# Layer 3 of a four-layer graph network on one core: constants made in layer 2, rank comparisons summed on TensorE, 1/std applied after the projection, blocks in a written-out order

## The chip, the core and the metric

The kernel runs on one core of a Trainium2 chip. The metric is the device time of the core in microseconds. Before the change the median of three runs is 767.4 us (766.89 to 767.92). The execution that the profiler recorded took 764.35 us, of which 762.5 us lie between its first and its last instruction (the span). The mean clock that TensorE was granted in it is 0.952 of full speed.

## The reference

Four layers work on `x` (2708 nodes, 128 features) and a 0/1 matrix `adj` (2708 x 2708). Each is `x = x + layer(relu(layernorm(x)))`. The first three (an attention layer, a graph convolution, a mean aggregation with batch normalisation) are not touched. The last one, with `X = relu(layernorm(x))`, is

```python
XW = jnp.matmul(X, W)
s_col = jnp.matmul(XW, a[0, :f])
s_row = jnp.matmul(XW, a[0, f:])
Z1 = jax.nn.leaky_relu(s_row[:, None] + s_col[None, :], negative_slope=0.01)
den = jnp.exp(Z1)
num = jnp.matmul(A, den)
att = jnp.where(num != 0, den / jnp.where(num != 0, num, 1.0), 0.0)
H = jnp.matmul(A, jnp.matmul(att, XW))
```

and layer normalisation is `(x - m) / sqrt(v + eps)` over the 128 features.

## The kernel before, in words

The nodes are cut into 22 tiles of 128 (the last has 20), and the tiles into six blocks of four (the last block has two). Layers 0 to 2 stream `adj` and its transpose and multiply on TensorE (PE) by block. Layers 1 and 2 are driven by a list of slots, four passes of 22 tiles: for each slot the kernel prepares a cast adjacency tile (L483 on VectorE, DVE; L481 on ScalarE, ACT), issues its matmuls (L614), and then runs whatever small steps were put at that tick (`put`, L498). In a slot of layer 2's first pass there are eight matmuls of 512 columns. All of it lies in an `in_order()` section (L236): within it each engine executes its instructions as the program writes them. Outside such a section a scheduler picks the order.

Layer 3 does not form the 2708 x 2708 exponentials row by row. It sorts nodes by their score `s_row` (in the code `r_of`), cuts the sorted order into chunks of 124, and takes sums of exponentials by chunk. So it needs the rank of each node: how many nodes have a larger score, ties broken by index. This is how the stage between layer 2 and the sorting works:

- Layer 2 ends with batch statistics: `tot` gets mean and variance (L833), 1/std (L834, a power on GpSimd, POOL, at L157), scale and offset (L835 to L837).
- Then come the constants of layer 3 (L862 to L912): five index patterns on POOL and some forty small instructions on DVE.
- `refresh(b)` (L990): ACT makes `z`, the normalised layer-2 result of a block (L997); PE turns it (L184); DVE adds it to `xs` (L1001); then `layernorm` (L164): statistics on DVE (L167, L168), 1/std by the power on POOL (L157), `shift` on DVE (L172), and the scaled and shifted relu `h` on ACT (L174).
- `project(b)` (L1012): PE turns `h` (L180), ACT copies it to `hT` (L1018), PE multiplies by the weight with two score columns (L1025, two tiles to a PSUM bank), ACT copies the scores `r_of` and `c_col` (L1026, L1027), takes `c_scale` = exp(0.01 c) (L1028) and scales the values `xw` (L1031), which SP stores (L1032). DVE spreads the scores onto a diagonal (`diag`, L1037), PE multiplies it by ones (L1044), and ACT copies the product to `row_b` (L1045): every partition then holds the scores of the whole block in a row.
- `ranks(b)` (L965): for each tile t of the block, DVE compares `row_b` of all earlier tiles with the tile's own scores (`bits`, L972; L978 for the first five, where DVE sums as well). For tiles after the fifth, ACT sums the bits by row in a pass of its own (`junk`, L974, into `rowsum`). PE sums the bits by column into `rk` with a weight that picks one row per block (L985).
- `diagonal(b)` (L953): the same within a tile, with the strict upper triangle `before`, the row sum read out into `tied` (L957), and the column sum on PE (L961).
- The scores are split into bf16 pieces (L1059), `rk` is copied and turned (L1083, L1086), `below` = others - rowsum - tied (L1087, L1088), and the rank is `below` plus the column count (L1092 to L1098). `less` (L1100), the weights `wts` (L1106, L1107), and the whole planning of chunks and gathers follow from the rank.

In this stage the scheduler, not the program text, sets the order. For instance it runs the `refresh` of all blocks well ahead of the projections. `bits` has three buffers, `bank` two PSUM banks; banks `acc0` to `acc5` are single.

Of the kernel before, what the change touches and what calls it, by code (L numbers as in the profile page):

```python
# [20 lines left out]
def binary(  # L21
# [21 lines left out]
    nc = tc.nc  # L43
# [675 lines left out]
    with in_order():  # L719
# [48 lines left out]

        lay_pool = tc.tile_pool(name="lay", bufs=2, side="right", reuse_waits="tile")
# [43 lines left out]

        NTAIL2 = 3
# [20 lines left out]
    nc.vector.tensor_mul(tot[:, 5:6], vecs[:, 2:3], tot[:, 4:5])  # L835
    nc.vector.scalar_tensor_tensor(tot[:, 2:3], tot[:, 0:1], -1.0, tot[:, 5:6], ALU.mult, ALU.mult)
    nc.vector.tensor_add(tot[:, 6:7], tot[:, 2:3], vecs[:, 3:4])  # L837

    CH = P - 4
    NC = T  # L840
    NE = T
    NS = 2 * NE
    NW = NC - 1
    NV = 5
    FAR_DOWN = float(1 << 16)
# [3 lines left out]

    const3 = ctx.enter_context(tc.tile_pool(name="const3", bufs=1, side="right"))  # L850

    def iota(name, shape, pattern, mult, base=0):
        o = const3.tile(shape, F32, name=name)
        nc.gpsimd.iota(o, pattern, base=base, channel_multiplier=mult, allow_small_or_imprecise_dtypes=True)
        return o

    def const_op(name, shape, op, *args, dtype=F32):
        o = const3.tile(shape, dtype, name=name)
        op(o, *args)
        return o  # L860

    node = iota("node", [P, T], [[P, T]], 1)  # L862
    by_ch = iota("by_ch", [P, NC + 1], [[CH, NC + 1]], 0)
    lane = iota("lane", [P, P], [[1, P]], 0)
    part = iota("part", [P, 1], [[0, 1]], 1)
    others = iota("others", [P, T], [[P, T]], -1, base=P - 1)
    nc.vector.tensor_scalar_add(others[:, TF:], others[:, TF:], float(TAIL - P))
    ts_ = nc.vector.tensor_scalar
    valid = const_op("valid", [P, T], ts_, node, float(N), None, ALU.is_lt)
    far = const_op("far", [P, T], ts_, valid, -1.0, 3.0e4, ALU.add, ALU.mult)  # L870
    lane_b = const_op("lane_b", [P, P], nc.vector.tensor_copy, lane, dtype=BF16)
    ones_b = const3.tile([P, P], BF16, name="ones_b")
    nc.vector.memset(ones_b, 1.0)
    before = const_op("before", [P, P], ts_, lane, part, None, ALU.is_gt, dtype=BF16)
    b_of = const3.tile([P, 1], F32, name="b_of")
    v_of = const3.tile([P, 1], F32, name="v_of")
    ge_v = const_op("ge_v", [P, NV], ts_, by_ch[:, :NV], float(NC) / CH, None, ALU.mult)
    nc.vector.tensor_tensor(ge_v, part.to_broadcast([P, NV]), ge_v, ALU.is_ge)
    nc.vector.tensor_reduce(v_of, ge_v[:, 1:], AX.X, ALU.add)
    nc.vector.scalar_tensor_tensor(b_of, v_of, float(-NC), part, ALU.mult, ALU.add)  # L880
    is_b = const_op("is_b", [P, NC], ts_, lane[:, :NC], b_of, None, ALU.is_equal)
    b_next = const_op("b_next", [P, P], ts_, ones, part, 1.0, ALU.mult, ALU.add)
    is_r = const_op("is_r", [P, 1], ts_, v_of, 3.0, None, ALU.is_lt)
    is_n = const_op("is_n", [P, 1], ts_, v_of, 3.0, None, ALU.is_ge)
    first = const3.tile([P, P], F32, name="first")
    nc.vector.memset(first, 0.0)
    nc.vector.memset(first[0:1, :], 1.0)
    joint = const3.tile([P, 2 * NC], F32, name="joint")
    nc.vector.memset(joint, 0.0)
    for i in range(3):  # L890
        row_of = small.tile([P, 1], F32, tag="row_of", name="row_of")
        ts_(row_of, part, float(1 - 2 * NW * i), None, ALU.add)
        hit = small.tile([P, 2 * NW], F32, tag="hit", name="hit")
        ts_(hit, lane[:, 1 : 2 * NW + 1], row_of, None, ALU.is_equal)
        nc.vector.tensor_add(joint[:, 1 : 2 * NW + 1], joint[:, 1 : 2 * NW + 1], hit)
    is_lo = const3.tile([P, 1], F32, name="is_lo")
    is_hi = const3.tile([P, 1], F32, name="is_hi")
    for o, m in ((0, is_lo), (1, is_hi)):
        ts_(m, part, float(CH + o), None, ALU.is_equal)
        two = const_op(f"two{o}", [P, 1], ts_, part, float(CH + 2 + o), None, ALU.is_equal)  # L900
        nc.vector.tensor_add(m, m, two)
    slope_hi = const_op("slope_hi", [P, 1], ts_, is_lo, -0.99, 1.0, ALU.mult, ALU.add)
    slope_lo = const_op("slope_lo", [P, 1], ts_, is_hi, 0.99, 0.01, ALU.mult, ALU.add)
    tiny = const3.tile([P, 1], F32, name="tiny")
    nc.vector.memset(tiny, 1e-18)
    up = const_op("up", [P, 1], ts_, part, float(NC), None, ALU.mult)
    pick_b = const3.tile([P, NB, NB], BF16, name="pick_b")
    nc.vector.memset(pick_b, 0.0)
    for b in range(NB):
        nc.vector.memset(pick_b[:, b, b : b + 1], 1.0)  # L910
    none_b = const3.tile([P, NB], BF16, name="none_b")
    nc.vector.memset(none_b, 0.0)  # L912
# [30 lines left out]
    r_of = row("r_of", T)  # L943
    c_col = row("c_col", T)
    c_scale = row("c_scale", T)
    rowsum = row("rowsum", T)
    nc.vector.memset(rowsum, 0.0)
    tied = row("tied", T)
    nc.vector.memset(tied, 0.0)
    rk = acc_bank(5)  # L950
    nc.tensor.matmul(rk[:NB, :], none_b, ones_b[:, None, :].to_broadcast([P, 4, P]), start=True, stop=False)

    def diagonal(b):  # L953
        for q, t in enumerate(TILES[b]):
            r = rows(t)
            own = tabs.tile([P, P], BF16, tag="own", name="own", bufs=4)
            nc.vector.scalar_tensor_tensor(  # L957
                own[:r, :r], row_b[:r, vcols(t)], r_of[:r, t : t + 1], before[:r, :r], ALU.is_ge, ALU.mult,
                accum_out=tied[:r, t : t + 1],
            )  # L960
            nc.tensor.matmul(  # L961
                rk[:NB, q * P : q * P + r], pick_b[:r, b, :], own[:r, :r], start=False, stop=(t == T - 1)
            )

    def ranks(b):  # L965
        for t in TILES[b]:
            if not t:
                continue
            r = rows(t)
            bits = tabs.tile([P, N], BF16, tag="bits", name="bits", bufs=3)  # L970
            if t > 5:
                ts_(bits[:r, : t * P], row_b[:r, : t * P], r_of[:r, t : t + 1], None, ALU.is_gt)  # L972
                junk = tabs.tile([P, N], BF16, tag="junk", name="junk", bufs=1)
                nc.scalar.activation(  # L974
                    junk[:r, : t * P], bits[:r, : t * P], AF.Identity, accum_out=rowsum[:r, t : t + 1]
                )
            else:
                ts_(  # L978
                    bits[:r, : t * P], row_b[:r, : t * P], r_of[:r, t : t + 1], None, ALU.is_gt, ALU.add,
                    accum_out=rowsum[:r, t : t + 1],  # L980
                )
            for k in range(NB):
                x0, x1 = E0[k][0], min(E0[k][1], t * P)
                if x1 > x0:
                    nc.tensor.matmul(rk[:NB, : x1 - x0], pick_b[:r, k, :], bits[:r, x0:x1], start=False, stop=False)  # L985
        diagonal(b)

    h3s, xws3 = {}, {}

    def refresh(b):  # L990
        lo, hi = E0[b]
        n = len(TILES[b])
        ts = tiles_of(b)
        z = tabs.tile([P, 512], F32, tag="z", name="z")
        if hi - lo < n * P:
            nc.gpsimd.memset(z[:, hi - lo :], 0.0)
        nc.scalar.activation(z[:, : hi - lo], row_b[:, lo:hi], AF.Relu, bias=tot[:, 6:7], scale=tot[:, 5:6])  # L997
        p = acc_bank(b % 2)
        turned_flat(p, z, b)
        f = len([t for t in TILES[b] if t < TF])  # L1000
        nc.vector.tensor_add(  # L1001
            xs[:, ts.start : ts.start + f, :].rearrange("p t d -> p (t d)"),
            xs[:, ts.start : ts.start + f, :].rearrange("p t d -> p (t d)"),
            p[:, : f * P],
        )
        if f < n:
            nc.vector.tensor_add(xs[:TAIL, TF, :], xs[:TAIL, TF, :], p[:TAIL, cols(f)])
        h3 = tabs.tile([P, 4, P], F32, tag="h3", name="h3")
        layernorm(b, h3)
        h3s[b] = h3  # L1010

    def project(b):  # L1012
        n = len(TILES[b])
        ts = tiles_of(b)
        p = acc_bank(2 + b % 2)
        turned(p, h3s.pop(b), b)
        hT = tabs.tile([P, 512], F32, tag="hT", name="hT")
        nc.scalar.copy(hT[:, : n * P], p[:, : n * P])  # L1018
        xw = tabs.tile([P, 4, P], F32, tag="xw", name="xw")
        for half in range(0, n, 2):  # L1020
            p = bank()
            us = slice(ts.start + half, ts.start + half + 2)
# [26 lines left out]
    for b in range(NB):  # L1049
        if b + 1 < NB:  # L1050
            refresh(b + 1)
        project(b)
        if b:
            ranks(b - 1)
# [978 lines left out]
```

## Time and profile before

| | us |
|---|---|
| median of three runs | 767.4 |
| the profiled execution | 764.35 |
| its span | 762.5 |
| last product of layer 2 (L679) ends | 325.6 |
| `tot` is done on DVE (L837) | 329.8 |
| first comparison on DVE (L978) | 349.25 |
| last row sum on ACT (L974) ends | 391.7 |
| `below` (L931 for L1087) starts | 391.75 |
| first gather of layer 3's main loop (L1380) | 418.97 |

Over the whole span PE is busy 655.9 us (86%), DVE 588.8 (77%), ACT 467.7 (61%), POOL 243.8 (32%). These shares are means over stages with different limits; the stage of the change lasts from 325.6 to 391.75 us, 9% of the span, and is to be read from stretches of its own. Times in the trace count from the span's start. A matmul's recorded time includes its tail, so matmuls in a row overlap: what one costs is the distance from start to start. A line can be a helper's: L859, for instance, stands for most constants, and L931 for every `tt(...)`. In a timeline, equal instructions in a row are merged and shown with their number (x5), and the time is that of the group.

### The profile page before, as it was taken

The page shows a single profiled execution, that of the slowest core. Times are in us where ns is not written, and L with a number is a line of the kernel's source. Part 1 is how long each engine was busy: PE and PEld are TensorE (multiplying, and loading weights), DVE is VectorE, ACT ScalarE, POOL GpSimd, SP SyncE. Part 2 cuts the span into 40 slices and gives each one's busy share as a digit, 9 for nine tenths or more (in the row PEclk, how much of TensorE's full clock was granted, in tenths as well). Part 3 has the DMA queues.
Part 4 walks back from the last instruction along what each step waited for, and adds up shares of the span by engine and source line. Part 5 has one row for each costly group of instructions (what it writes and reads, how often), then busy time and mean ns, then how long its engine had stood idle before and what let it go on. Part 6 is the DMA issues. An engine that isn't in the chain of part 4 may idle for free. (4 is left out here: it accounts for less than half of the span.)

```text
span 762.5 us, 8134 instructions
## 1 busy us (share of the span) xinstructions
PE 655.9 (86%) x2626; PEld 411.8 (54%) x2626; DVE 588.8 (77%) x1102; ACT 467.7 (61%) x702; POOL 243.8 (32%) x201
## 2 busy tenths in 40 slices
PE   5889888888899989858739848899999999999995
PEld 3433333335778767634317525566655666557784
DVE  5999778968857874677789758678897887867972
ACT  5666677648956744447960139678766777664442
POOL 3320000141101100021000547788787787500000
PEclk9999999999999999968979969999999999999997
DMA  9699999577442899001000425556766555758702
GB/s 335 259 395 420 426 424 395 216 266 280 158 185 60 308 344 330 0 1 41 29 7 1 116 76 153 161 155 166 168 148 177 146 146 137 167 204 317 268 27 63
DMA packets 49733, 146.27 MB, mean 192 GB/s; under 512 B 13602, under 2 KB 28446, under 8 KB 41254
## 3 DMA queue, kind: packets, MB, share of 16 engines
q1 hardware_dynamic: 28966, 85.11, 31.5%
q0 software_dynamic: 16032, 25.83, 12.7%
q10 hardware_dynamic: 4684, 34.73, 12.6%
q8 instruction: 23, 0.38, 0.2%
q14 instruction: 28, 0.23, 0.1%
HBM read 126.81 MB, written 18.77 MB: 191 GB/s over the span
## 5 line engine op out<-in xcount | busy, mean ns | idle before, releaser
L1512 PE MATMUL bank<-r,d_hi 128*128 128x512 f32 (+1 forms) x264 | 143.7, 549 | 20.2 <-DMA r<-pre_d,pre_i 11.1
L1513 ACT ACTIVATE ln<-bank,tiny 128x512 f32<-128x512 f32 x132 | 83.8, 635 | 66.7 <-DVE e L1491 37.6
L1466 PE MATMUL acc<-e,xw 128*128 128x512 f32 (+1 forms) x264 | 121.5, 548 | 0.0
L340 PE MATMUL acc<-tau,hw 128*128 128x512 f32 (+1 forms) x240 | 101.1, 566 | 12.9 <-DVE tau L348 12.8
L1512 PE MATMUL bank<-r,d_lo 128*128 128x512 f32 (+1 forms) x264 | 99.2, 380 | 0.0
L1458 DVE CAST r<-g 124x2708 fp32r<-124x2708 fp8e4 x44 | 69.4, 1612 | 35.7 <-issue 17.1
L1380 POOL DMA_INDIRECT g<-adjt_d,row_i x44 | 84.5, 1921 | 39.1 <-DVE row_i L1304 26.0
L481 ACT CAST m<-a 128x660 fp32r<-128x660 fp8e4 (+1 forms) x45 | 55.2, 1234 | 51.9 <-PE acc L1628 31.6
L1512 PEld LDWEIGHTS bank<-r,d_hi 128*128 128x128 f32 x264 | 51.0, 193 | 62.2 <-issue 32.1
L340 PEld LDWEIGHTS acc<-tau,hw 128*128 128x128 f32 x240 | 43.8, 194 | 71.6 <-issue 46.5
L348 DVE SCALAR_TENSOR_TENSOR tau<-row_b,sg,a 128x1536 f32<-128x1536 f32 (+1 forms) x44 | 70.7, 1623 | 10.7 <-DMA a<-in_adj_dram 9.9
L1380 POOL DMA_INDIRECT r<-pre_d,pre_i x44 | 63.6, 1445 | 40.8 <-PE bank L1512 19.5
L1491 DVE SCALAR_TENSOR_TENSOR e<-row_b,sig,ln 128x1536 f32<-128x1536 f32 (+3 forms) x46 | 71.4, 1559 | 6.1 <-PE bank L1512 4.5
L371 ACT ACTIVATE a<-a 128x2708 fp8e4<-128x2708 f32 x22 | 54.1, 2459 | 23.1 <-issue 10.9
L695 DVE SCALAR_TENSOR_TENSOR chk<-chk 128x2708 f32<-128x2708 f32 (+1 forms) x22 | 65.7, 2987 | 3.0 <-DMA chk<-in_adj_t_dram 3.0
L1512 PEld LDWEIGHTS bank<-r,d_lo 128*128 128x128 f32 x264 | 51.1, 194 | 28.5 <-issue 24.2
L157 POOL TENSOR_TENSOR rstd<-isq,neg_half 128x4 f32<-128x4 f32 (+1 forms) x24 | 27.9, 1164 | 117.1 <-DVE isq L156 96.3
L1485 ACT ACTIVATE ln<-ln 128x512 f32<-128x512 f32 (+2 forms) x68 | 62.8, 926 | 0.7 <-ACT ln L1513 0.7
L483 DVE CAST m<-a 128x2048 fp32r<-128x2048 fp8e4 (+1 forms) x43 | 39.5, 920 | 23.1 <-PE acc L614 12.9
L1466 PEld LDWEIGHTS acc<-e,xw 128*128 128x128 f32 x264 | 48.1, 190 | 12.7 <-issue 3.8
L614 PE MATMUL acc<-m,y_hi 128*128 128x512 f32 (+1 forms) x132 | 49.8, 384 | 5.6 <-DVE m L600 2.0
L614 PE MATMUL acc<-m,h_hi 128*128 128x512 f32 (+1 forms) x132 | 53.9, 415 | 0.1
(440 smaller groups left out, 1251.0 us busy)
## 6 DMA issues: line engine op xcount, KB each, us to landing
a<-in_adj_dram SPq DMA_DIRECT2D x21, 1354.0 KB
adjt<-in_adj_t_dram ACTq DMA_DIRECT2D x12, 1354.0 KB
chk<-in_adj_t_dram ACTq DMA_DIRECT2D x11, 1354.0 KB
chk<-in_adj_t_dram SPq DMA_DIRECT2D x10, 1354.0 KB
a<-in_adj_t_dram SPq DMA_DIRECT2D x9, 1354.0 KB
adj_d<-a POOLq DMA_DIRECT2D x22, 338.5 KB
adjt_d<-adjt SPq DMA_DIRECT2D x5, 1354.0 KB
a<-adj_d SPq DMA_DIRECT2D x5, 1024.0 KB
```

What stands on the lines that cost most here:

```text
L340: nc.tensor.matmul(accs[b][:, : hi - lo], stationary, tau[b // 3][:, o : o + hi - lo], start=first, stop=last)
L348: nc.vector.scalar_tensor_tensor(tau, row_b[:, h0:h1], sg[:, t : t + 1], tiles_a[t][:, h0:h1], ALU.max, ALU.mult)
L481: nc.scalar.copy(m[:, : hi - lo], src[:, lo:hi])
L614: nc.tensor.matmul(sums_of[phase, b][:, : hi - lo], part[:, t, :], tiles_m[k][:, lo - base : hi - base], start=t == 0 and i == 0, stop=t = ...
L695: lambda: nc.vector.scalar_tensor_tensor(a[:r], a[:r], 1.0, a[:r], ALU.is_equal, ALU.not_equal, accum_out=odd[:r, t : t + 1])
L1380: return nc.gpsimd.indirect_dma_start(out=out, out_offset=None, in_=src, in_offset=bass.IndirectOffsetOnAxis(ap=idx, axis=0),)
L1458: ins = nc.vector.tensor_copy(rows_r[q][:CH], g[:CH])
L1466: m = nc.tensor.matmul(ys_acc[b][:, : hi - lo], xws[s], waiting[s][:, lo:hi], start=(s == 0), stop=(s == NE - 1))
L1485: pin(nc.scalar.activation(lns[s][:, lo:hi], lns[s][:, lo:hi], AF.Exp, scale=-1.0))
L1491: nc.vector.scalar_tensor_tensor(waiting[s][:, lo:hi], row_b[:, lo:hi], sig[:, s : s + 1], lns[s][:, lo:hi], ALU.max, ALU.mult)
L1512: pin(nc.tensor.matmul(num[:, : hi - lo], d, a[:, lo:hi], start=(i == 0), stop=(i == 3)))
L1513: pin(nc.scalar.activation(lns[s][:, lo:hi], num[:, : hi - lo], AF.Ln, bias=tiny))
```

## The change

Four things are done.

1. The constants of layer 3 are put into layer 2's slots: `later` collects one instruction each, and `put(l2_tick + 2 + i, make)` places one at each tick from layer 2's first pass on. `first` goes, a bf16 identity `ident_b` is new.
2. 1/std of the last layer normalisation no longer scales `h`. `centred` takes relu(x - mean) only, and 1/std is multiplied into the scores (`scores`, on DVE, straight from PSUM) and into the values' factor (`factors`: the exponential on ACT, a multiplication on POOL, then `values3` on ACT). The copies of `r_of` and `c_col` on ACT go.
3. The row sums of the comparisons go to PE. `compared(t)` writes the strict and the diagonal comparison into one `bits` tile; PE adds it up by column as before, and then adds its t+1 pieces of 128 columns onto each other with `ident_b` as the weight, in one PSUM bank (`folds`, acc3) for the four tiles of a block. `row_sums(b)` on DVE reduces that bank. The ACT pass, the sums on DVE and `tied` go.
4. The whole stage stands in an `in_order()` section, whose order is written out. The explicit load of the activation table ahead of the stage goes.

The diff, cut to its core:

```diff
+        later = []
...
+        def const_op(name, shape, op, *args, dtype=F32):
+            o = cell(name, shape, dtype)
+            later.append(lambda: op(o, *args))
+            return o
...
+        ident_b = const_op("ident_b", [P, P], nc.vector.tensor_copy, ident, dtype=BF16)
...
+        for i, make in enumerate(later):
+            put(l2_tick + 2 + i, make)
...
-    rk = acc_bank(5)
-    nc.tensor.matmul(rk[:NB, :], none_b, ones_b[:, None, :].to_broadcast([P, 4, P]), start=True, stop=False)
-    def diagonal(b):
...
-    def ranks(b):
...
-                nc.scalar.activation(
-                    junk[:r, : t * P], bits[:r, : t * P], AF.Identity, accum_out=rowsum[:r, t : t + 1]
-                )
...
+        nc.vector.tensor_scalar_mul(shift[:, ts], mv[:, ts, 0], -1.0)
+        inv_sqrt(rstd[:, ts], mv[:, ts, 1], 1e-5)
+
+    def centred(b):
+        hs3[b] = h3 = tabs.tile([P, 4, P], F32, tag="h3", name="h3")
+        for q, t in enumerate(TILES[b]):
+            nc.scalar.activation(h3[:, q, :], xs[:, t, :], AF.Relu, bias=shift[:, t : t + 1])
...
+    def scores(b):
+        ts = tiles_of(b)
+        for i, pv in enumerate(ps3[b]):
+            us = slice(ts.start + 2 * i, ts.start + 2 * i + 2)
+            nc.vector.tensor_tensor(
+                rc[:, us, :], pv[:, :, P:], rstd[:, us, None].to_broadcast([P, 2, 2]), ALU.mult
+            )
...
+    def factors(b):
+        ts = tiles_of(b)
+        nc.scalar.activation(c_scale[:, ts], c_col[:, ts], AF.Exp, scale=0.01)
+        nc.gpsimd.tensor_tensor(factor[:, ts], c_scale[:, ts], rstd[:, ts], ALU.mult)
...
+    def compared(t):
+        b, q = divmod(t, 4)
+        r = rows(t)
+        bits = tabs.tile([P, N], BF16, tag="bits", name="bits", bufs=3)
+        if t:
+            ts_(bits[:r, : t * P], row_b[:r, : t * P], r_of[:r, t : t + 1], None, ALU.is_gt)
+        nc.vector.scalar_tensor_tensor(
+            bits[:r, vcols(t)], row_b[:r, vcols(t)], r_of[:r, t : t + 1], before[:r, :r], ALU.is_ge, ALU.mult
+        )
...
+        if q == 0:
+            folds[b] = acc_bank(3)
+        for s in range(t + 1):
+            c = vcols(s)
+            w = c.stop - c.start
+            nc.tensor.matmul(
+                folds[b][:r, q * P : q * P + w], ident_b[:r, :r], bits[:r, c], start=s == 0, stop=s == t
+            )
+
+    def row_sums(b):
+        full = [t for t in TILES[b] if t < TF]
+        p = folds.pop(b)
+        nc.vector.tensor_reduce(
+            rowsum[:, full[0] : full[-1] + 1],
+            p[:, : len(full) * P].rearrange("p (t q) -> p t q", q=P),
+            AX.X,
+            ALU.add,
+        )
...
+    with in_order():
...
+        relu_z(0)
+        turn_z(0)
+        relu_z(1)
+        refresh(0)
+        turn_z(1)
+        centred(0)
+        turn_h3(0)
+        for b in range(NB + 1):
+            todo = list(TILES[b - 1]) if b else []
+            if b < NB:
+                project(b)
+            if todo:
+                compared(todo.pop(0))
+            if b < NB:
+                scores(b)
+                factors(b)
+                diag_of(b)
+                broadcast_r(b)
+            if b + 2 < NB:
+                relu_z(b + 2)
+                turn_z(b + 2)
+            if b < NB:
+                values3(b)
+            if b + 1 < NB:
+                refresh(b + 1)
+                centred(b + 1)
+            if todo:
+                compared(todo.pop(0))
+            if todo:
+                compared(todo.pop(0))
+            if b + 1 < NB:
+                turn_h3(b + 1)
+            while todo:
+                compared(todo.pop(0))
+            if b:
+                row_sums(b - 1)
...
     below = tt("below", [P, T], others, rowsum, ALU.subtract)
-    nc.vector.tensor_sub(below, below, tied)
```

In the changed kernel's numbering the fold is L1081, the column count L1073, the comparisons L1065 and L1066, `row_sums` L1088, the copy to `row_b` L1039.

## The prediction

> **What bounds the kernel now.** I read the table of stretches first, because the change touches one stage only: between layer 2's last product (325.6 us) and the ranks of layer 3. Columns: stretch, its length, busy us of PE, PEld, DVE, ACT, POOL (instructions), granted clock, DMA share, GB/s.
>
> ```profile
> 330.00:340.00 10.00, 6.48 (x25) 4.06 (x25) 7.76 (x64) 6.50 (x12) 2.39 (x3) 0.67 0.01 2
> 340.00:350.00 10.00, 7.43 (x30) 5.45 (x31) 6.60 (x44) 8.65 (x35) 3.72 (x4) 0.74 0.09 26
> 360.00:370.00 10.00, 7.69 (x38) 4.09 (x38) 7.09 (x19) 9.94 (x28) 0.00 (x0) 0.95 0.09 26
> 370.00:380.00 10.00, 8.60 (x37) 3.29 (x37) 7.79 (x18) 9.68 (x23) 0.00 (x0) 0.87 0.10 29
> 380.00:390.00 10.00, 5.49 (x30) 2.18 (x27) 8.14 (x32) 10.00 (x14) 0.00 (x0) 0.98 0.04 13
> ```
>
> From 360 on ScalarE is full, VectorE three quarters busy, TensorE half to four fifths, DMA idle. The timelines of ACT and DVE then show where the stage ends (start, length, engine, line, operation; in brackets the idle time before and its releaser).
>
> ```profile
> 389.19 2.44 ACT L974 ACTIVATE junk<-bits 20x2688 bf16<-20x2688 bf16 x1
> 391.54 0.19 ACT L974 ACTIVATION_READ_ACCUMULATOR junk<-bits 20x1 f32 x1
> 391.75 0.18 DVE L931 TENSOR_TENSOR below<-others,rowsum 128x22 f32<-128x22 f32 x1 [1.41 <-ACT junk L974]
> 391.97 0.18 DVE L1088 TENSOR_TENSOR below<-below,tied 128x22 f32<-128x22 f32 x1
> ```
>
> ScalarE's row-sum pass L974 releases `below`; VectorE and TensorE had finished near 390. All that follows (ranks, planning, gathers from 419) hangs on `below`, with no DMA of its own to meet, so I move it rigidly. The start of the stage, same view:
>
> ```profile
> 329.90 1.52 ACT L997 ACTIVATE z<-row_b,tot 128x512 f32<-128x512 f32 x2 [7.24 <-DVE b_of L880]
> 337.07 1.65 ACT L174 ACTIVATE h<-xs,shift,rstd 128x128 f32<-128x128 f32 x4 [1.12 <-DVE shift L172]
> 347.24 0.59 ACT L1045 COPY row_b<-acc 128x512 f32<-128x512 f32 x1 [1.05 <-PE acc L1044]
> 349.25 0.34 DVE L978 TENSOR_SCALAR_CACHE_REDUCE bits<-row_b,r_of 128x128 bf16<-128x128 f32 x1
> ```
>
> So 19.3 us pass before the first comparison, 42 us in comparing. Prices for what is added:
>
> ```profile
> 357.33 1.12 PE L1044 MATMUL acc<-diag,ones 128*128 128x512 f32 x2
> 360.69 1.16 PE L1025 MATMUL bank<-w_ext,hT 128*128 128x130 f32 x8
> 383.30 1.24 PE L985 MATMUL acc<-bits,pick_b 128*6 128x512 bf16 x5 [0.18 <-DVE bits L972]
> 416.16 1.43 PE L1299 MATMUL bank<-lanes_k,rhs_k 128*110 128x128 bf16 x22
> 379.44 1.49 DVE L972 TENSOR_SCALAR bits<-row_b,r_of 128x2432 bf16<-128x2432 f32 x1 [0.19 <-ACT junk L974]
> 417.07 0.66 DVE L1259 TENSOR_REDUCE at<-place 128x22 f32<-128x484 f32 x1
> ```
>
> The first four are TensorE's, at full clock; the last matmul tail (0.38, 0.22) taken off, a 512-column count costs (1.24-0.38)/4 = 0.215 us and a 128-column one (1.43-0.22)/21 = 0.058.
>
> **The Trainium skill.** "TensorE: Matmul & The Clock Gate", section "Wait — 56ns, not 53.3ns?", gives 215.7 and 55.6 ns for these two; the trace agrees. Its section "Part 1: The HAM clock gate" says that an idle TensorE falls to half clock and needs some 3.4 us of work to leave it; here the granted clock is 0.50 from 340 to 344 and eight L1025 matmuls take 2.10 there instead of 1.16. Its section "Architectural detail" says that ACT and DVE queues are strict first-in first-out; the trace agrees (at 281.3 DVE waited 1.78 us for a `chk` load with a small `shift` behind it, which ran only at 286.04). This last decides my forecast.
>
> **The change, part by part.**
> *Constants.* 43 small DVE instructions and 5 POOL iotas leave 325.8 to 331.9. On the path they held two waits for iotas (0.34 and 0.38 us) and small work ahead of `tot`. I put `tot` at 329.0 instead of 329.8 (bounds 328.7 and 329.8). In layer 2 they take about 43 x 0.09 = 3.9 us of DVE over 28 us in which DVE is some 75% busy and TensorE paces; most hide in DVE's waits for POOL's 1.0 us power. Where that cover is gone they delay a `shift`, ACT's `y` and TensorE's turn behind it. Bounds: -0.3 (other slots) to +2.5; I take +0.5. `first` and the table load (1.28 us in ACT's idle time at 321) go for nothing; the built order has one load, at the start.
>
> *1/std moved.* `h` no longer waits for POOL's power. First block: `z` at 329.05; as before 2.02 to the `xs` addition; addition 0.60, stats 0.85, aggregates 0.4, `shift` 0.2: `h` at 333.2 (337.07 before). Four `h` 1.65, last turn 0.4, `hT` 0.6, projection at half clock 2.1, scores and `diag` 1.0, broadcast at half clock 2.0, copy 0.6, latencies 0.2: `row_b` of block 0 at 341.8, against 347.83. That is 6 us earlier. The added POOL multiply (not in the trace: 0.3 to 1.0, the power being the top; 0.45 taken) is done under the next `z` (0.8 on ACT); uncovered it would add at most 0.5 in two blocks. The `xw` stores stay six, SP idle around them.
>
> *Row sums on TensorE.* ACT loses 16 passes, some 27 us; TensorE gains t+1 matmuls per tile, 253 in all: 253 x 0.058 = 14.7 us. With the counts (0.215/4 = 0.054 per 128 columns) a tile costs TensorE 0.111(t+1). DVE loses the `tied` read-out: the diagonal's 0.275 from start to start becomes about 0.22 (not under 0.16, which rows of one column take; not over 0.30); it gains six reduces of about 0.65 (L1259's 0.66; top 1.17, a strided reduce at 398). Comparison: 0.14 + 0.067t.
>
> *Fixed order, and the new wait.* `row_sums` of a block stands in DVE's queue before the first comparison of the next block, and waits for TensorE's last fold. Behind it are scores, `diag`, `xs`, stats, so the next projection's use; TensorE in turn waits for these comparisons. So per block, with first tile a, times add up: DVE first tile 0.36 + 0.067a; scores, `diag`, `xs`, four stats, four aggregates, `shift`, `isq` with waits 3.2; second tile 0.43 + 0.067(a+1); then TensorE's pairs for three tiles, 0.111(3a+9), with the turn of `h` and latency 0.75; reduce 0.68.
> Block 0 is set by ACT instead: from 341.8, `z` 0.8, `xw` 1.1, `h` 1.6, turn and `hT` 1.0, projection 2.1, scores and `diag` 1.0, broadcast 2.0, copy 0.6 (351.9), again `z`, `xw`, `h` 3.5, turn 0.3, pair of tile 3 0.5, reduce 0.7: 356.9.
> a=4: 0.63+3.2+0.77+3.08+0.68 = 8.4. a=8: 0.90+3.2+1.03+4.41+0.68 = 10.2. a=12 (next block half size, 2.6 and 0.55): 11.3. a=16 (only scores and `diag`, 0.9; 0.3): 1.43+0.9+1.57+6.63+0.68 = 11.2. Last, tiles 20 and 21: 1.70, pairs 2.33 and 2.40, 0.3, two short reduces 0.5: 7.2. Together 48.3, so `below` at 405.2 against 391.75: +13.4; one `tied` subtraction less, -0.2; layer 2 +0.5. Sum +13.7.
> The profiled execution took 764.35 (span 762.5 and 1.85 around it), 3 us under the median 767.4; the sum gives 778.0 for it and 781.1 for a median: I predict 781.
>
> **Rivals.**
> 1. *The engines overlap, faster.* After 341.8 TensorE has about 27 us of pairs, 5.6 projection, 5 broadcast, 4.5 turns, 42 to 43 in all at full clock; DVE 18.4 + 4.8 + 3.7 + 13 = 40. Without gaps `below` comes at 385.5: 767.4 - 6.4 + 0.5 = 761.5. For it: ACT, the bound, is freed, and three `bits` buffers let DVE run ahead. Against: the reduce in DVE's queue stops it six times. It decides when TensorE's gaps after 341.8 stay under some 6 us; I count about 20. In-between cases end from 762 to 775.
> 2. *Half clock goes on.* TensorE idles 1 to 3 us in each block; before, after two such gaps (348, 366) the clock fell to 0.5 for 3.4 us. If it falls in most blocks, pairs double (+20 us): about 800. Each single fall costs 1.7. For it: gaps; against: long dense runs from tile 8 on.
> 3. *Layer 2 pays.* The constants delay the check at 267, its buffer, the next load and the stall of 2.95 us on L180 at 286: the full 2.5, giving 783.
>
> **How the numbers follow.** Forecast 0.71, its own range 775 (full clock from 330: -3.8, and cheap diagonals) to 787 (two clock falls +3.4, layer 2 +2.0). Rival 1 0.12, of it 0.02 within 0.2%; rival 2 0.10; rival 3 0.07. The range 771 to 789 leaves out most of rivals 1 and 2, 0.17. A measurement here can tell about 0.2% (1.5 us) from no change. Faster 0.10, same 0.02, slower 0.88.
>
> **What would show it.** Right: first `row_b` near 342; DVE idle 2 to 3 us before each L1088, released by PE L1081; L1081 at 58 ns a piece; `below` near 405; ACT under half busy from 360. Wrong: `below` before 392, or L1088 without a wait, or folds well under 58 ns. Layer 2 is wrong if its last product moves by over 2.5 us.

## The result and the profile after

The changed kernel takes 780.5 us (median of four runs, 780.35 to 781.03), the kernel before 767.7 (four runs, 766.9 to 769.4): a ratio of 1.0166 (95% interval 1.0148 to 1.0184), 12.9 us slower. The forecast was 781.

The profiled execution of after took 780.45 us with a span of 778.6, that of before 764.35 with 762.5. These spans differ by 16.1 us, the medians by 12.9, since the profiled execution of before lay 3 us under its median. The 16.1 us are found so: layer 2's last product ends 0.69 us later (326.29 against 325.60); the stage from there to the start of `below` grew from 66.15 to 80.89 us, by 14.74; from `below` to the end it is 371.4 against 370.75, 0.65 more.

The same stretches of after (columns as in the table of before: PE, PEld, DVE, ACT, POOL, granted clock, DMA share, GB/s):

```profile
340.00:350.00 10.00, 7.12 (x21) 3.92 (x20) 3.43 (x17) 4.27 (x12) 1.41 (x2) 0.50 0.10 28
360.00:370.00 10.00, 7.21 (x57) 4.22 (x57) 7.68 (x32) 5.18 (x15) 1.99 (x4) 1.00 0.09 26
370.00:380.00 10.00, 8.73 (x75) 5.36 (x76) 7.55 (x21) 3.27 (x12) 2.58 (x3) 1.00 0.10 28
380.00:390.00 10.00, 8.02 (x80) 5.03 (x80) 7.02 (x17) 2.88 (x11) 2.02 (x2) 1.00 0.10 29
390.00:400.00 10.00, 7.79 (x82) 4.84 (x80) 8.20 (x28) 0.90 (x3) 0.00 (x0) 1.00 0.05 13
```

ScalarE, full before, is half busy and then nearly idle. But no engine is full: from 360 to 400 PE and DVE each leave 13 to 30% of every stretch unused, which is what two engines look like that wait for each other in turn. DVE's timeline shows where it waits (time idle before, and releaser, in brackets):

```profile
356.55 0.69 DVE L1088 TENSOR_REDUCE rowsum<-acc 128x4 f32<-128x512 f32 x1 [3.96 <-PE acc L1081]
...
365.37 0.69 DVE L1088 TENSOR_REDUCE rowsum<-acc 128x4 f32<-128x512 f32 x1 [2.19 <-PE acc L1081]
...
375.45 0.69 DVE L1088 TENSOR_REDUCE rowsum<-acc 128x4 f32<-128x512 f32 x1 [2.38 <-PE acc L1081]
...
386.37 0.69 DVE L1088 TENSOR_REDUCE rowsum<-acc 128x4 f32<-128x512 f32 x1 [2.94 <-PE acc L1081]
...
397.83 0.69 DVE L1088 TENSOR_REDUCE rowsum<-acc 128x4 f32<-128x512 f32 x1 [1.76 <-PE acc L1081]
...
406.67 0.29 DVE L1088 TENSOR_REDUCE rowsum<-acc 128x1 f32<-128x128 f32 x1 [0.51 <-PE acc L1081]
...
407.18 0.18 DVE L938 TENSOR_TENSOR below<-others,rowsum 128x22 f32<-128x22 f32 x1
```

The reduce of each block comes up in DVE's queue and stands there until PE has folded the block's last tile; nothing behind it on DVE starts before. Its six waits sum to 13.7 us. And PE's timeline shows the other half, once with a consequence:

```profile
396.50 1.29 PE L1081 MATMUL acc<-bits,ident_b 128*128 128x128 bf16 x20
400.03 2.40 PE L1073 MATMUL acc<-bits,pick_b 128*6 128x512 bf16 x6 [2.25 <-DVE bits L1065]
402.37 1.86 PE L1081 MATMUL acc<-bits,ident_b 128*128 128x128 bf16 x21
404.15 1.30 PE L1073 MATMUL acc<-bits,pick_b 20*6 20x512 bf16 x6
```

PE had folded tile 19 and waited 2.25 us for tile 20's comparison, which stood behind the reduce on DVE and took 1.55 us itself. After that gap the six counts took 2.40 us, and 1.30 when they came again: the granted clock was 0.53, 0.50, 0.50 and 0.76 in the four microseconds from 400 on, and 1.00 before and after. "TensorE: Matmul & The Clock Gate" in the Trainium skill, section "Part 1: The HAM clock gate", puts one idle window of about 3.4 us ahead of half clock; here half clock followed a gap of 2.25 us. The 3.4 us of sustained work that the section asks for until full clock agree with the length of the slow stretch, 3.4 us by these figures.

### The profile page after: what moved, and what is told of

Same layout as the page of the kernel before. It is cut to its first block, busy times and chain, and to the rows that moved or that the text cites. A ratio compares the mean times of both kernels' runs of the same rounds, so it can differ in the third digit from the quotient of the medians.

```text
span 778.6 us, 8510 instructions
## 1 busy us (share of the span) xinstructions
PE 670.9 (86%) x2863; PEld 426.0 (55%) x2863; DVE 592.9 (76%) x1090; ACT 438.5 (56%) x642; POOL 246.0 (32%) x207
## 4 chain that ended last, share of the span: by engine, by line
PE 31%; DMA 19%; DVE 17%; issue 16%; ACT 6%; POOL 5%; ACTq 0%; POOLq 0%; DVEq 0%
DMA g<-adjt_d,row_i 9%; PE acc L1711 7%; PE acc L614 5%; PE bank L1595 4%; PE acc L1549 4%; DMA chk<-in_adj_t_dram 4%; DVE chk L695 3%; DVE r L1541 2%; DMA r<-pre_d,pre_i 2%; DMA adj_d<-a 2%; PE acc L1073 2%; PE acc L1081 2%; ACT adjt L216 2%; PE acc L1206 2%; POOL r L1463 1%
## 5 line engine op out<-in xcount | busy, mean ns | idle before, releaser
L1463 POOL DMA_INDIRECT g<-adjt_d,row_i x44 | 86.4, 1964 | 40.2 <-DVE row_i L1387 27.1
L1463 POOL DMA_INDIRECT r<-pre_d,pre_i x44 | 61.6, 1400 | 43.5 <-issue 22.2
L157 POOL TENSOR_TENSOR rstd<-isq,neg_half 128x4 f32<-128x4 f32 (+1 forms) x24 | 30.8, 1285 | 124.8 <-DVE isq L156 98.6
```

What stands on the lines that cost most here:

```text
L1463: return nc.gpsimd.indirect_dma_start(out=out, out_offset=None, in_=src, in_offset=bass.IndirectOffsetOnAxis(ap=idx, axis=0),)
```

## The experiments

My theory was: the written-out order makes one chain of DVE's and PE's work in every block, and this chain is the loss; the folds are not too dear in themselves, and layer 2 pays nothing. Rivals: layer 2 pays for the constants; the folds cost their time in any order; the reduce's wait alone is the loss.

The runs were made on other occasions than the pair above, so each is compared by its ratio to the kernel before that ran beside it, and by its own stage: from the end of layer 2's last product (L679) to the start of `below`, in its profiled execution. Each stage is thus one execution. Where kernels run the same steps in the same order it repeats well: the first `row_b` is done 15.5 to 15.6 us after the last product in after, e2, e4, e5 and e8.

| kernel | stage, us | ratio to before (95%) |
|---|---|---|
| before | 66.15 | 1 |
| after | 80.89 | 1.0166 (1.0148 to 1.0184) |
| e1_const | 62.23 | 0.9991 (0.9967 to 1.0015) |
| e2_folds_twice | 94.16 | 1.0388 (1.0328 to 1.0448) |
| e3_no_order | 59.19 | 0.9939 (0.9912 to 0.9966) |
| e4_sums_on_act | 87.46 | 1.0266 (1.0215 to 1.0317) |
| e5_sums_late | 76.14 | 1.0150 (1.0098 to 1.0201) |
| e6_scale_only | 60.97 | 0.9950 (0.9918 to 0.9982) |
| e7_split | 53.03 | 0.9858 (0.9819 to 0.9898) |
| e8_two_first | 73.24 | 1.0149 (1.0103 to 1.0195) |

### e1_const: the constants alone

The kernel before, with the constants' lines moved into `later` as in the change; layer 3's stage is unchanged.

```diff
+        for i, make in enumerate(later):
+            put(l2_tick + 2 + i, make)
```

> The kernel before with the constants alone made in layer 2. My theory (the stage's fixed order costs the time, the constants about nothing): layer 2's last product 0.7 us later than 325.6, tot 0.5 us earlier against the product's end, so below within 1 us of 391.75 and the time at 767.9 (766.5 to 769.3). Rival 3 (layer 2 pays): 770 to 771.

Measured: 764.9 us against 765.3 beside it, ratio 0.9991. Layer 2's last product ended at 325.10 (before: 325.60). The traces say more: from the first product with `h_hi`, ahead of which none of the constants is made, to the last product it is 82.65 us in before and 81.5 to 82.8 in the nine kernels with the constants. Rival 3, layer 2 pays, is out. The stage was 3.9 us shorter, where I had expected at most 1: `row_b` of the first block was done 18.6 us after the last product instead of 22.2. The small instructions are out of DVE's way there, and the order is chosen anew; the run doesn't separate the two. Most of this is not seen in the time; see the last paragraph of this part.

### e2_folds_twice: the folds doubled

```diff
-        for s in range(t + 1):
+        for s in list(range(t + 1)) * 2:
```

> The changed kernel with each tile's fold issued twice (the second set starts the sums anew, so the output stays the same): 253 more matmuls of 0.055 us, 13.9 us of TensorE. My theory (three quarters of the pairs lie on each block's chain): 11 to 12 us more than the changed kernel, about 792, below near 418. If the engines overlapped and TensorE had slack: at most 3 us more, about 783. If the folds only hurt through the clock: less gap on TensorE, no clock fall, 778 to 785.

Measured: 793.8 us, ratio 1.0388; by the ratios 2.2% or 17 us more than after (about 4 uncertain), the stage 13.3 us longer for 13.9 us of matmuls. So nearly all of the added folds' time is on the path of the fixed order, more than my three quarters; there is no slack on PE. The waits of DVE up to 416 us (five of the six) say the same, here with their sum, their number and the longest:

```profile
DVE rowsum L1088 <- PE acc L1081: 24.1, 5, 5.9
```

In after this line read 13.7, 6, 4.0.

### e3_no_order: the same operations, ordered by the scheduler

```diff
-    with in_order():
+    if True:
         nc.vector.tensor_scalar_mul(tot[:, 2:3], tot[:, 0:1], -1.0)
```

> The changed kernel with the fixed order around layer 3's first stage taken away, so that the scheduler orders it as it did before the change; same operations. My theory (the order makes the chain): below 8 to 14 us earlier than 407.2, the time 766 to 773. Rival (TensorE's folds cost their 14.7 us in whatever order): 778 to 782. In the built order the six row-sum reduces still stand inside the next block's comparisons, so some waits of 1 to 2 us on them stay.

Measured: 761.9 us, ratio 0.9939; 2.2% or 17 us under after, and below the kernel before. `below` started at 385.45, 21.7 us earlier than in after, where I had expected 8 to 14, with all 253 folds and all six reduces still there. The stretches of this kernel:

```profile
340.00:350.00 10.00, 9.43 (x58) 4.99 (x56) 8.74 (x33) 7.57 (x25) 1.95 (x4) 0.99 0.18 52
360.00:370.00 10.00, 10.00 (x97) 6.11 (x95) 8.50 (x18) 2.88 (x9) 3.00 (x2) 1.00 0.09 26
370.00:380.00 10.00, 10.00 (x101) 6.25 (x101) 9.97 (x35) 1.82 (x7) 1.00 (x1) 1.00 0.06 16
```

PE is full where in after it was busy 72 and 87%, and at full clock already from 340 to 350 (0.99, in after 0.50). The reduces hardly wait (1.6 us in three waits). Why, is seen where ACT copies each block's scores to `row_b`; first e3_no_order, then after:

```profile
342.03 0.60 ACT L1039 COPY row_b<-acc 128x512 f32<-128x512 f32 x1
345.14 0.59 ACT L1039 COPY row_b<-acc 128x512 f32<-128x512 f32 x1
350.20 0.59 ACT L1039 COPY row_b<-acc 128x512 f32<-128x512 f32 x1 [0.33 <-PE acc L1036]
356.76 0.59 ACT L1039 COPY row_b<-acc 128x512 f32<-128x512 f32 x1
364.65 0.59 ACT L1039 COPY row_b<-acc 128x512 f32<-128x512 f32 x1 [0.31 <-PE acc L1036]
375.17 0.37 ACT L1039 COPY row_b<-acc 128x256 f32<-128x256 f32 x1 [2.16 <-PE acc L1036]
```

```profile
341.25 0.58 ACT L1039 COPY row_b<-acc 128x512 f32<-128x512 f32 x1 [2.71 <-PE acc L1036]
351.13 0.58 ACT L1039 COPY row_b<-acc 128x512 f32<-128x512 f32 x1 [2.65 <-PE acc L1036]
359.98 0.58 ACT L1039 COPY row_b<-acc 128x512 f32<-128x512 f32 x1 [1.70 <-PE acc L1036]
369.07 0.58 ACT L1039 COPY row_b<-acc 128x512 f32<-128x512 f32 x1 [1.71 <-PE acc L1036]
379.77 0.59 ACT L1039 COPY row_b<-acc 128x512 f32<-128x512 f32 x1 [2.06 <-PE acc L1036]
390.97 0.37 ACT L1039 COPY row_b<-acc 128x256 f32<-128x256 f32 x1 [1.57 <-PE acc L1036]
```

The first block is done at the same moment. But the scheduler turns and normalises the later blocks while PE would idle (`h` of the second block starts at 336.80, in after at 343.45), so the second follows after 3 us instead of 10, and comparisons are hardly waited for. In the fixed order each block's scores wait for the turn in which they stand. That the folds cost their 14.7 us in any order is out. The clock has a share in the 21.7 us: in after's second block the turns, the projection and the broadcast took 1.11, 1.34, 2.10 and 2.08 us at half clock, and 0.66, 0.60, 1.11 and 1.13 at full clock later. By estimate the differences make 3 us, with 1.7 more for the fall at 400. No run separates it from the order.

### e4_sums_on_act: the fixed order kept, the row sums given back to ScalarE

```diff
+        if b:
+            junk = tabs.tile([P, N], BF16, tag="junk", name="junk", bufs=1)
+            nc.scalar.activation(junk[:r, :hi_t], bits[:r, :hi_t], AF.Identity, accum_out=rowsum[:r, t : t + 1])
+            return
         if q == 0:
             folds[b] = acc_bank(3)
...
-            if b:
-                row_sums(b - 1)
+            if b == 1:
+                row_sums(0)
```

> The changed kernel, fixed order kept, but the row sums of blocks 1 to 5 back on ScalarE as one pass over each tile's comparison bits (block 0 keeps its folds). My theory (the order is what costs; a schedule worked out by hand from the changed kernel's durations): 404 instead of 407 for below, the time 777 to 781. Rival (the folds and the reduce's wait cost it): their share gone, the time at 766 to 770.

Measured: 786.1 us, ratio 1.0266; the stage is 6.6 us longer than after's. That is against the rival (folds to blame), but my own number missed too: I had worked with full clock. Its stretches:

```profile
360.00:370.00 10.00, 5.92 (x24) 3.37 (x24) 5.42 (x20) 8.13 (x19) 1.44 (x2) 0.86 0.08 26
370.00:380.00 10.00, 7.72 (x22) 2.23 (x20) 7.29 (x21) 6.75 (x16) 2.47 (x3) 0.63 0.09 26
380.00:390.00 10.00, 8.54 (x26) 3.74 (x27) 6.22 (x17) 6.11 (x14) 2.67 (x2) 0.66 0.03 10
390.00:400.00 10.00, 5.39 (x16) 2.22 (x15) 4.94 (x12) 7.92 (x14) 0.27 (x1) 0.73 0.06 18
```

Without folds PE idles more, and the granted clock is 0.63 to 0.86 where after had 1.00, so that what was left for PE took longer too. Why it idles, its waits from 356 to 416 us say (sum, number, longest):

```profile
PE bank L1007 <- ACT hT L1001: 10.0, 3, 4.6
```

In after this wait does not occur in the same stretch. ACT's passes stand in its queue ahead of the copy of `hT`, for which the next projection waits; the order lets a slow ACT hold PE as it lets PE hold DVE. At the end an activation of a later step (L1460, 2.44 us) ran ahead of the last two passes, for whose end `below` waited 5.71 us. How the 10 us of the miss divide among clock, `hT` and L1460 wasn't tried. The folds, which the rival blamed, are thus cheaper in this order than the passes that they replace.

### e5_sums_late: the reduce without its wait

```diff
-            folds[b] = acc_bank(3)
+            folds[b] = acc_bank(3 + b % 2)
...
-        p = acc_bank(4)
+        p = acc_bank(2)
...
                 centred(b + 1)
+            if b > 1:
+                row_sums(b - 2)
...
-            if b:
+            if b == NB:
                 row_sums(b - 1)
```

> The changed kernel, fixed order, with two fold banks in place of one (the broadcast shares the turns' bank) and each block's row-sum reduce moved behind the next block's first comparison, scores, diag, statistics, where the folds are long done: the 13.7 us of waits on L1081 all but gone. If these waits themselves cost their time (rival): below 8 to 12 us earlier than 407.2, about 768 to 772. My theory (the wait only hides that DVE's other work and TensorE's pairs stand in one chain; without the reduce's wait DVE waits for the next projection instead): 3 us earlier, 776 to 779, and rc's wait on L1007 grows by most of what the reduce's wait loses.

Measured: 777.7 us, ratio 1.0150, whose interval holds after's 1.0166, so the time alone tells nothing. The stage is 4.75 us shorter than after's, nearer to my 3 than to the rival's 8 to 12. Most of this comes at the end: tile 19's folds start 69.4 us after the last product, in after 70.2. Behind them after has its gap of 2.25 us and its fall of the clock, e5_sums_late has neither. The waits of DVE from 342 to 408 us, in after and then in e5_sums_late:

```profile
DVE rowsum L1088 <- PE acc L1081: 13.7, 6, 4.0
DVE rc L1014 <- PE bank L1007: 5.7, 2, 5.1
```

```profile
DVE rc L1014 <- PE bank L1007: 14.2, 9, 5.1
DVE bits L1065 <- PE acc L1081: 1.7, 1, 1.7
...
DVE rowsum L1088 <- PE acc L1081: 0.5, 1, 0.5
```

The 13.2 us that the reduce no longer waits come back to two thirds as waits of the scores (L1014, 8.5 us more) for the next projection, which stands in PE's queue behind the same folds. The wait of L1088 is thus where the chain shows, not what the chain is.

### e6_scale_only: constants and 1/std, without folds and without the fixed order

The changed kernel with `ranks`, `diagonal` and `tied` of before in place of `compared`, the folds and `row_sums`, the calls in the program order of before, and no ordered section. The change had also put `hT`, `diag` and the bank for the turns of `h` from two buffers to one; here they have two again (and `diag` of a later step has one more).

```diff
-    with in_order():
...
+                nc.scalar.activation(
+                    junk[:r, : t * P], bits[:r, : t * P], AF.Identity, accum_out=rowsum[:r, t : t + 1]
+                )
```

> The kernel before (its row sums on ScalarE, its order left to the scheduler) with the constants in layer 2 and with 1/std applied to projected scores and values: the change without folds and without the fixed order. My theory: a gain, since ScalarE, the bound there, loses the score copies and exps (about 4 us), the scale in h (22 x 0.09 = 2 us) and starts 1 to 2 us earlier: below near 381, 757 to 761. If the gain of 1/std is hidden (ScalarE's passes start no earlier): within 1.5 us of e1_const, 764 to 766.

Measured: 762.6 us, ratio 0.9950; faster than before, but not told apart from e1_const by its interval, and its stage is only 1.3 us shorter than e1's. `below` started at 388.00, not 381. ACT's groups from 326 to 392 us show that the work did shrink: `h` took 7.3 us instead of e1's 10.1, and the copies of `r_of` and `c_col` (2.0 and 2.1 us of busy time, mostly overlapped) are gone. It was spent at the end:

```profile
380.64 2.44 ACT L1441 ACTIVATE row_b<-row_b 128x2708 f32<-128x2708 f32 x1
382.99 2.32 ACT L1084 ACTIVATE junk<-bits 128x2560 bf16<-128x2560 bf16 x1
385.21 0.19 ACT L1084 ACTIVATION_READ_ACCUMULATOR junk<-bits 128x1 f32 x1
385.43 2.44 ACT L1084 ACTIVATE junk<-bits 20x2688 bf16<-20x2688 bf16 x1
```

Here the scheduler put L1441, a step that nobody waits for yet, ahead of the last two passes, which set `below`. In e1_const the same step (2.44 us) came after them. So 2.4 us of the gain went to the order once more, and 1.4 of the 7 us are only a later last product (327.03 against 325.60); the rest, some 3 us, stays open.

### e7_split: no fixed order, row sums shared by PE and ACT

Program order and scheduler as in e6_scale_only, `hT` and `diag` with two buffers as there; `row_sums(b)` reduces only the block's folded tiles.

```diff
-    with in_order():
+    FOLD = [t for t in range(TF) if t < 4 or t % 4 < 2]
...
+        if t not in FOLD:
+            junk = tabs.tile([P, N], BF16, tag="junk", name="junk", bufs=1)
+            nc.scalar.activation(junk[:r, :hi_t], bits[:r, :hi_t], AF.Identity, accum_out=rowsum[:r, t : t + 1])
+            return
```

> The changed kernel without the fixed order (as e3_no_order) and with the row sums shared: folds for 13 tiles (123 matmuls instead of 253, 6.8 us), ScalarE's pass for the other nine tiles (16.5 us on an engine that was a third busy). My theory: TensorE, full in e3_no_order from 345 to 383, is relieved by 7 us, VectorE (also near full) by 2 us, so below 2 to 4 us earlier than 385.5 and the time 756 to 761. If TensorE alone had bound e3_no_order: 6 us earlier. If ScalarE's passes delay what the next block waits for (as in e4_sums_on_act): later than e3_no_order.

Measured: 755.5 us against 766.1 beside it, ratio 0.9858: 1.4% faster than before and 3% faster than after. `below` started at 379.72, 5.7 us before that of e3_no_order, and the stage is 6.2 us shorter. I had expected 2 to 4; 6 was the number for TensorE alone as the bound of e3_no_order. The run can't decide this, since buffers and program order differ from e3_no_order too.

```profile
350.00:360.00 10.00, 9.59 (x59) 4.60 (x57) 9.97 (x33) 9.47 (x23) 1.68 (x3) 1.00 0.10 28
360.00:370.00 10.00, 9.72 (x79) 5.88 (x80) 9.50 (x19) 6.83 (x16) 1.59 (x3) 1.00 0.17 52
370.00:380.00 10.00, 8.36 (x69) 4.34 (x67) 9.46 (x34) 9.75 (x12) 2.60 (x2) 1.00 0.05 16
```

Three engines are near full at once, and the clock stays. This is the version that the experiments point to: the constants, 1/std and half of the folds are together worth 1.4% without the fixed order. What each is worth alone the times don't tell: the intervals of e1_const and e6_scale_only overlap, and so do those of e6_scale_only and e3_no_order.

### e8_two_first: one comparison moved within the fixed order

The diff is against e5_sums_late.

```diff
-            if todo:
-                compared(todo.pop(0))
+            for t in todo[:2]:
+                compared(t)
+            todo = todo[2:]
             if b < NB:
                 scores(b)
```

> e5_sums_late with one thing moved in the fixed order: the second comparison of a block stands ahead of the next block's scores on every engine, instead of behind its statistics. If TensorE and VectorE wait for each other in turn because of where the calls stand (my theory), TensorE now has one tile's counts and folds more to do while VectorE does scores, diag and statistics: a schedule worked out by hand gives 4.8 us less than e5_sums_late, below near 399.6 (against a last product near 327.5), 772 to 775. Rival (the depth of one block, not the place of the calls, sets the pace): within 1.5 us of e5_sums_late, 776 to 779.

Measured: 773.8 us, ratio 1.0149. The ratio doesn't tell it from e5_sums_late. Its stage is 2.9 us shorter, between the two expectations (4.8 and at most 1.5), nearer to neither in a way that settles it: the place of a call counts, but less than I worked out. From after over e5 and e8 to e3_no_order the stage goes 80.9, 76.1, 73.2, 59.2; what the last 14 us consist of, call by call, wasn't tried. Part of it precedes all row sums: from the last product to the second `row_b` it takes 25.1 us in e8 and 19.5 in e3.

**What stays open.** Beyond `below` all kernels run nearly the same program, yet the profiled executions took 366 to 377 us for it (after 371.4, e1 373.1, e3 377.1, e6 366.3). In e3 PE waited 8.2 us for three gathered tiles between 500 and 562 us, in before 0.7. Whether an earlier stage makes these gathers meet more, or single executions merely differ, can't be told from one profile of each; so 22 us of e3's stage became 17 in time, and 4 us of e1's hardly 1.

## Why the prediction was right

Step by step, predicted and then measured in after's trace (us):

| step of the prediction | predicted | measured |
|---|---|---|
| layer 2 pays for the constants | +0.5 | +0.69 |
| `tot` done | 329.0 | 329.35 |
| first `h` | 333.2 | 333.52 |
| first `row_b` done | 341.8 | 341.83 |
| reduce of block 0 done | 356.9 | 357.24 |
| then, a=4 | 8.4 | 8.82 |
| a=8 | 10.2 | 10.08 |
| a=12 | 11.3 | 10.92 |
| a=16 | 11.2 | 11.46 |
| tiles 20 and 21, to `below` | 7.2 | 8.66 |
| `below` | 405.2 | 407.18 |

The predicted times of day leave out the 0.5 us of layer 2. With it `below` was due at 405.7, and the 1.5 us that were missing are the last tiles'. So the mechanism held step by step, and the last digits of 781 are luck: the sum said 13.7 us, the two profiled executions differ by 16.1 and the medians by 12.9.

- *Bound.* That ACT's row sums set `below` before, and that all behind it moves rigidly, held: from `below` to the end 0.65 us more, in a difference of 16.1.
- *Constants.* Layer 2 hid them, more fully than said. The +0.69 of after is not their cost: its first product with `h_hi` came 1.85 us later than in before, ahead of all constants, and from there layer 2 took 1.16 us less. What I left out is that the same move is worth 3.9 us of stage in a kernel that the scheduler orders.
- *1/std.* The first `row_b` came 6.0 us earlier, as worked out, but not for the reason given alone: counted from the last product it took 22.2 us in before, 18.6 with the constants moved (e1_const), 16.1 with 1/std moved as well (e6_scale_only) and 15.5 in after. Without the fixed order 1/std was worth 1.3 us of stage over the constants, some 5.5 less than e6's expectation; 2.4 of these went to L1441, the rest is open. The added POOL multiply took 0.40 us (0.45 assumed), and nobody waited for it.
- *Row sums on TensorE.* A fold cost 0.056 us from start to start at full clock (20 folds took 1.29 us and six 0.51; predicted 0.058); the 55.6 ns of the Trainium skill's "TensorE: Matmul & The Clock Gate", section "Wait — 56ns, not 53.3ns?", agree. The diagonal, taken at 0.22 us, cost 0.26 from start to start: 22 x 0.04 = 0.9 us of DVE, partly hidden.
- *Fixed order and the new wait.* This decided it, and the sums by block were right within 0.5 us but for the last. The waits ahead of L1088 were 1.8 to 4.0 us, released by L1081 as named, and 0.5 for the last. The experiments sharpen the cause: I had written that the reduce in DVE's queue stops it six times. That is true, but e5_sums_late, which takes these waits away, wins only 4.75 of 21.7 us; it is the whole order that binds (e3_no_order), and in it added folds cost what they take (e2_folds_twice).
- *The last tiles.* The term that was too small: 7.2 us became 8.63, because PE's clock fell once after its gap of 2.25 us. Six counts took 2.40 instead of 1.30 and 21 folds 1.86 instead of about 1.3, some 1.7 us. Rival 2 had this price for a single fall, 1.7; it happened once after 356, not in most blocks.
- *Rival 1.* The overlap that would have made it faster was set at `below` = 385.5. With the scheduler's order it exists: 385.45 in e3_no_order. So the bound by engine work was about right. Against it I had named the reduce in DVE's queue, and this is only a part of what kept after from it: the fixed order as a whole did.

## What to carry to other kernels

Before a stage's order is written out by hand, sum for each block what one engine does while the next waits for it; where two engines stand still in turn, each at three quarters, the order can cost more than any operation in it (here 21.7 us of stage, the folds being 14.7 us of work), and the same operations without it may be a gain. A wait that a profile shows at one instruction can move to the next when it is taken away there; ask who waits for the same engine. And work taken from TensorE need not come back as time: in e4_sums_on_act, without most folds, it idled more and its clock was 0.63 to 0.86.

## What was not expected of the hardware

- A gap of 2.25 us on PE (397.8 to 400.0) was followed by half clock for 3.4 us; gaps of 1.39, 1.08 and 1.47 us (before 361.3, 370.1 and 388.3) were not. From 330 to 355 us after stayed at 0.50, although PE's records cover more than half of each 2 us from 340 on; e3_no_order, denser from 336 on, had full clock from about 340. What share of work decides wasn't measured.
- ACT's small copies (128x2) take 0.16 to 0.26 us each in before but follow one another after 0.05, so that removing 22 of them removes some 1 us of ACT by estimate (22 x 0.05), not the 4.1 of their busy time in e1_const.
- `h` (128x128) without a scale operand from memory started every 0.29 us (four took 1.28, one 0.40), with one every 0.39 (1.65 and 0.49).
